# A channel gate between two LSTMs: statistics spread by TensorE, its 24 comparisons divided over VectorE, GpSimd and ScalarE

## The chip, the cores and the metric

The kernel runs on one core of a Trainium2 chip. The metric is the device time of one execution in microseconds (us). The five engines are named as in the profile: PE is TensorE (its weight loads are listed apart, as PEld), DVE is VectorE, ACT is ScalarE, POOL is GpSimd and SP is SyncE, which here only starts transfers.

## The reference

The input is a batch of 4 images with 256 channels of 64 x 64 pixels in float32. Two layers follow each other. The first adds a deformable 3 x 3 convolution of the normalized input and then an LSTM of width 256 over the pixels (`c_new = h * c + i * g`, three gates), which runs along the images' tokens. The second adds a gate over channels and again an LSTM. The change is about the gate of the second layer and the seams on both of its sides:

```python
def _L1_conv_ref(x, w, gamma, beta, running_mean, running_var):   # x: the normalized y, (b, c, h, w)
    b, c, h, wd = x.shape
    xf = x.reshape(b, c, h * wd)
    mean = xf.mean(-1)
    mx = xf.max(-1)
    std = jnp.std(xf, axis=-1, ddof=1)
    u = jnp.stack([mean, mx, std], axis=-1)
    med = jnp.median(u.reshape(b, -1), axis=-1)
    u = (u - med[:, None, None]) ** 3
    z = jnp.einsum('bck,ck->bc', u, w)
    z = (z - running_mean) * jax.lax.rsqrt(running_var + BN_EPS) * gamma + beta
    g = jax.nn.sigmoid(z)
    return x * g[:, :, None, None]

# --- layer 1 ---
x = x + _L1_conv_ref(_ln_c(x), ...)
t = _to_tokens(x)
t = t + _L1_ffn_ref(_ln_t(t), ...)
```

`_ln_c` normalizes each pixel over its 256 channels. For each image there are 256 x 3 = 768 statistics, and their median is needed before any gate can be computed. So the gate needs all of the first LSTM's output, and the second LSTM needs the gate.

## The kernel before

**Tiling.** The pixels of four images are cut into 128 tiles (`NTILE`), each of 128 lanes (32 for each image) by 256 channels. Each image's sequence of tokens is cut into 32 pieces that run side by side, one in each lane, so that one step of the LSTM handles one tile. A piece starts from a state that is guessed by some steps over the end of the piece before it; that the guess agrees with the state really reached is checked afterwards (`count_held`). `ORDER` (line 539) lists 144 steps: 16 that only warm the state up (`WARM`; of these the first 4, `FIRST`, are left out), and then the 128 tiles. Both the warm-up steps 4 to 15 and the last 12 steps (132 to 143) handle tiles 116 to 127.

**Order.** `Ordered` and `InOrder` (lines 391 to 430) tie each instruction to the one that the program issued before it on the same engine. The order in the code is therefore the order on every engine.

**First stage.** `sample_and_recur` (line 578) runs the sampling of the convolution, the first LSTM and the gate's statistics in numbered slots. The 576 (`PAIRS`) slots of sampling come first; the last steps of the LSTM go on for some 75 slots after that. In a slot each engine gets its fixed part (`core`), and then work from a list (`Spare`) that has become due and for which there is room. When two finished tiles of the LSTM have been normalized over channels (`styled`, line 857), ScalarE writes y and y squared into a buffer (`style`), VectorE adds both to sums over lanes (`lanes`) and takes the maximum (`highest`). Before slot 592 these buffers come from the pool "y", after it from `squares`: 40 tiles of 256 numbers that held the sampled rows, and that are used as 10 slots of four tiles. `free` lists the slots that can be had, and `highest` gives a slot back. The last pair, steps 142 and 143, goes through `ending` (line 902), in which TensorE adds up the sums over lanes into `pq`. `Gate.scaled` works out gamma divided by the square root of the running variance at slot 288.

**Gate.** `Gate.gates` (line 1429) follows the last step:

- It makes `u`, 128 lanes x 4 images x 6 numbers (two halves of the channels, three statistics). The lane is the channel.
- SyncE writes `u` to DRAM (`ud`) and reads each image's 768 numbers back to all 128 lanes (`ubs`, in the first 12 tiles of `squares`). Behind these five transfers in SyncE's queue stand loads for the second LSTM (`ring<-x2d`).
- Meanwhile ScalarE normalizes the 12 tiles 116 to 127 again, from `ring`, into `early` (line 1478), and VectorE runs `meanwhile()`: this is `count_held` (line 1097).
- Then, for each image and each of the 6 columns, the number of the 768 values that are not above the lane's own is counted. `OWN = 4` columns of each image are counted by VectorE, with one compare whose accumulator gives the count. For 2 columns ScalarE runs a sign and a square, each with an accumulator, and two small VectorE instructions turn these into the count (`net`, `both`, `le`).
- `idle` products with no use keep TensorE busy (`turn_over`): 4 of them from the next to last compare on, 10 behind the gate's last product.
- From the counts VectorE picks the candidates for the median, GpSimd takes the maximum over lanes (`partition_all_reduce`), and a few VectorE instructions lead to `z`. ScalarE takes the sigmoid, VectorE spreads it over each image's 32 lanes (`G2`), two products with the identity turn it over into PSUM (`pg`), and VectorE copies that to `gb`.

**Second stage.** `gated_lstm` (line 1115) is the second layer. `gated` (line 1147) multiplies the normalized tile by `gb`, adds it to the tile and takes statistics; for the first 12 tiles the normalized values are those in `early`. It begins with four tiles (line 1256 and after), their norm, and the first transposes (`xt`) on TensorE.

All of the waits above come from the tiles: the framework makes an instruction wait for the producers of what it reads and for the readers of what it overwrites.

Of the kernel before, what the change touches and what calls it, by code (L numbers as in the profile page):

```python
# [11 lines left out]
F32 = mybir.dt.float32  # L12
I32 = mybir.dt.int32
AF = mybir.ActivationFunctionType
ALU = mybir.AluOpType
# [4 lines left out]
P = 128  # L20
B, C, H, W = 4, 256, 64, 64
T = H * W
NC = C // P
# [63 lines left out]
def normalize(nc, out, x, rs, low, j, f=AF.Identity):  # L87
    nc.scalar.activation(out, x, f, scale=rs[:, j : j + 1], bias=low[:, j : j + 1])
# [489 lines left out]
def sample_and_recur(  # L578
# [241 lines left out]
        give("DVE", slot, 0.9 if n0 < LAST else 2.2, begin, urgent=n0 >= LAST, soon=lo < NB)  # L820


    now, free = {"slot": 0}, [*range(SQUARES)]
    taken = {"xn": 0, "y": 0, "ms": 0, "ys": 0, "cm": 0}

    def room(tag, n):
# [30 lines left out]
    def styled(b, p, slot):  # L857

        n = b * NB + 2 * p
        y, k = result(slot)  # L860
# [12 lines left out]

    def result(slot):

        if slot > PAIRS + 16:
            k = free.pop(0)
            return squares[:, 4 * k : 4 * k + 4].rearrange("p (q i) c -> p q i c", q=2), k
        taken["y"] += 1
        return yp.tile([P, 2, 2, C], F32, name="y", tag="y"), None  # L880

    def style(y, n, i):
        t = ORDER[n + i]
# [3 lines left out]
    def highest(y, k):  # L887
        nc.vector.tensor_max(gate.mx, gate.mx, y[:, 0])
        if k is None:
            taken["y"] -= 1  # L890
        else:
            free.append(k)

    def lanes(n, y, k, slot):
# [7 lines left out]
    def ending(slot):  # L902

        n = STEPS - 2
        (y, _), (both, _) = result(slot), result(slot)
# [8 lines left out]
        highest(y, 0)  # L914


    def step_slot(n):
# [137 lines left out]
    while s <= step_slot(STEPS) or not spare.empty():  # L1055
# [35 lines left out]
        if s + AHEAD < PAIRS:  # L1091
            gather(s + AHEAD)
        s += 1
    return lambda: count_held(nc, st, cnt, ((state["cell"], state["cguess"]), (state["h"], state["hguess"])))


def count_held(nc, st, cnt, pairs):

    for i, (end, guess) in enumerate(pairs):
        d = st.tile([P, NC, P], F32, name="dif", tag="hc")  # L1100
        nc.vector.tensor_sub(d, end, guess)
        nc.vector.tensor_mul(d, d, d)
# [12 lines left out]
def gated_lstm(tc, pools, const, weights, src, dst, cnt, gate):  # L1115
# [5 lines left out]
    nc = Ordered(tc.nc, pools["after"])  # L1121
    ident = const[0]
    Us, Vs, bs = weights
    rs_y, low_y, gb, early = gate
# [22 lines left out]
    def gated(b, j):  # L1147

        if b >= NBATCH:
            return  # L1150
        t, x = ORDER[b * NB] + j, ring[:, (b + 1) % 4, j]
        lo, hi = part(b, j)
        if j == lo:
            sts[b, lo] = sm.tile([P, 20, 6], F32, name="st", tag="sth")[:, : hi - lo]
        if b < 2:
            d = early[:, b * NB + j - FIRST]
        elif (b, j) in styles:
            d = styles.pop((b, j))
        else:
            d = yp.tile([P, C], F32, name="d", tag="y")  # L1160
            normalize(nc, d, x, rs_y, low_y, t)
        nc.vector.tensor_mul(d, d, gb)
        nc.vector.tensor_add(x, x, d)
        nc.vector.bn_stats(sts[b, lo][:, j - lo], x)

# [132 lines left out]
    def style(b, lo, n):  # L1298

        for j in range(lo, lo + n):  # L1300
            d = styles[b, j] = early[:, (b * NB + j - FIRST) % (2 * NB - FIRST)]
            normalize(nc, d, ring[:, (b + 1) % 4, j], rs_y, low_y, ORDER[b * NB] + j)

    def turned_over(b, p):
# [73 lines left out]
    put(*last)  # L1378
    assert not adds
    store(last[0], NB // 2, NB)  # L1380
    count_held(nc, st, cnt, ((cell, cguess), (h, hguess)))


class Gate:
# [15 lines left out]

    def scaled(self, nc, gamma, rvar):
        nc.vector.tensor_scalar(rvar, rvar, 1e-5, None, ALU.add)
        nc.vector.tensor_mul(self.params[1], gamma, inv_sqrt(nc, self.pools["small"], rvar, NC))

    def begin(self):
        nc = Ordered(self.tc.nc, self.pools["after"])
# [19 lines left out]
                        skip_group_check=True,  # L1426
                    )

    def gates(self, meanwhile):
# [8 lines left out]
        def each(v, n):  # L1438

            return v.unsqueeze(1).to_broadcast([P, B, n])  # L1440
# [22 lines left out]


        uf = u.rearrange("p i k s -> p i (k s)")
        ud = self.pools["dram"].tile([B, P * NU], F32, name="ud", tag="ud")
        nc.sync.dma_start(ud.rearrange("i (p s) -> p i s", s=NU), uf)
        ubs = []
        for i in range(B):
            ubs.append(space[:, i * P * NU : (i + 1) * P * NU])  # L1470
            nc.sync.dma_start(ubs[i], ud[i : i + 1].to_broadcast([P, P * NU]))


        OWN = 4
        minus = wk.tile([P, B, NU - OWN], F32, name="minus", tag="minus")
        nc.scalar.activation(minus, uf[:, :, OWN:], AF.Copy, scale=-1.0)

        early = self.pools["squares"][:, 3 * (B + 3) : 3 * (B + 3) + 2 * NB - FIRST]
        for n in range(FIRST, 2 * NB):
            normalize(nc, early[:, n - FIRST], self.pools["ring"][:, NB + n], self.rs, self.low, ORDER[n])  # L1480
        meanwhile()
        le = wk.tile([P, B, NU], F32, name="le", tag="le")
        net = wk.tile([P, B, NU - OWN], F32, name="net", tag="net")
        both = wk.tile([P, B, NU - OWN], F32, name="both", tag="both")
        cmp, *sgs = (space[:, i * P * NU : (i + 1) * P * NU] for i in range(B, B + 3))
        for i, ub in enumerate(ubs):
# [303 lines left out]
def metaformer_kernel(ctx: ExitStack, tc: tile.TileContext, a: dict, out: bass.AP):  # L1790
# [10 lines left out]
    with ExitStack() as main:  # L1801
# [53 lines left out]
        def gate_weights(queue):  # L1855
# [14 lines left out]
        held = sample_and_recur(  # L1870
            tc, pools, const, wconv, a["x"], table, plan, x1, x2, weights[0], cnt[:, 0], gt, *errands
        )
        gated_lstm(tc, pools, const, weights[1], x2, out, cnt[:, 1], gt.gates(held))


    held = fp.tile([P, 1], F32, name="held")
# [65 lines left out]
```

## Time and profile before

| | |
|---|---|
| median of 6 runs | 3088.23 us (3081.8 to 3092.93) |
| the profiled execution | 3090.72 us |
| its span in the profile | 3088.5 us |
| granted TensorE clock, mean | 0.987 of full speed |
| PE, PEld, DVE, ACT, POOL busy | 97%, 90%, 86%, 66%, 50% of the span |
| end of the sampling, by the last gather | 2153 us |
| last step of the first LSTM, its h | 2280.0 us |
| statistics `u` complete | 2291.66 us |
| first compare, last compare's end | 2299.01 us, 2315.88 us |
| first product with the gate | 2321.12 us |
| first transposes of the second LSTM | 2329.85 us |

Times inside the execution are counted from the start of the span. A line of the timeline gives the start, the length, the engine, the source line (420 for nearly all, since a helper issues them), the operation, the tile it writes and those it reads, the shapes, how many such instructions were merged, and in brackets how long the engine sat idle before it and what ended that. A group of instructions has its total, the mean of one in ns, and the idle time before them. The share of busy time over the whole span says little here: the gate is some 40 of 3088 us, and has limits of its own.

### The profile page before, as it was taken

The numbers are of one execution on the slowest core, as the hardware profiler recorded it, in microseconds if no ns is written. First come the engines' busy times: TensorE is split into PE (matmuls) and PEld (weight loads), VectorE is DVE, ScalarE is ACT, GpSimd is POOL, SyncE is SP. The second block draws the span as 40 slices with busy tenths as digits, with TensorE's granted clock in tenths as the row PEclk, the third lists the DMA queues.
The fourth block names the chain that finished last, engine by engine and source line by source line (L and its number), as shares of the span: only waits on it lengthen the run. The fifth ranks groups of instructions, "written<-read, shape, count | busy, mean of one in ns | idle before, by whom it ended". The sixth has DMA issues, their size and how long they took to land.

```text
span 3088.5 us, 61571 instructions
## 1 busy us (share of the span) xinstructions
PE 2992.6 (97%) x20252; PEld 2791.7 (90%) x20252; DVE 2669.2 (86%) x7864; ACT 2049.1 (66%) x5414; POOL 1552.0 (50%) x1577
## 2 busy tenths in 40 slices
PE   7978999999999999999999999999969999999998
PEld 6967999999999999999999999999968999999997
DVE  6768998989999999999999999999677777777774
ACT  6746566666777767767677777777775666666653
POOL 3357665555666666666666666666000123223221
PEclk9989999999999999999999999999979999999999
DMA  9999999999999999999999999998110245444442
GB/s 311 321 337 344 345 318 335 332 332 327 325 330 329 333 332 317 342 331 321 334 331 332 330 333 331 322 331 304 59 62 28 79 154 156 150 153 144 147 139 85
DMA packets 316024, 816.02 MB, mean 264 GB/s; under 512 B 100392, under 2 KB 104488, under 8 KB 313392
## 3 DMA queue, kind: packets, MB, share of 16 engines
q0 software_dynamic: 188288, 669.62, 62.1%
q1 hardware_dynamic: 124240, 139.95, 13.4%
q8 instruction: 163, 2.67, 0.3%
q10 hardware_dynamic: 3168, 2.43, 0.2%
q14 instruction: 165, 1.35, 0.1%
HBM read 694.91 MB, written 116.94 MB: 263 GB/s over the span
## 4 chain that ended last, share of the span: by engine, by line
PE 86%; issue 6%; DMA 3%; DVE 3%; ACT 1%; SPq 0%; POOL 0%; DVEq 0%; ACTq 0%; POOLq 0%
PE acc L420 30%; PE ga L420 14%; PE gacc L420 8%; PE gtr L420 8%; PE tr L420 8%; PE gb L420 7%; PE gga L420 4%; PE ggb L420 4%; DMA squares<-table,plan 2%; PE zacc L420 1%; DVE v L420 1%; PE xt L420 1%; PE ht L420 1%; DMA squares<-in_x_dram 1%; PE zga L420 1%
## 5 line engine op out<-in xcount | busy, mean ns | idle before, releaser
L420 POOL DMA_INDIRECT squares<-table,plan x1152 | 1308.7, 1136 | 671.2 <-DVE v L420 150.8
L420 DVE SCALAR_TENSOR_TENSOR v<-squares,plan,v 128x256 f32<-128x256 f32 x3456 | 1412.8, 476 | 24.9 <-ACT v L420 23.4
L420 PE MATMUL acc<-wconv,vt 128*128 128x256 f32 x4608 | 1094.7, 380 | 16.4 <-ACT vt L420 16.3
L420 PEld LDWEIGHTS acc<-wconv,vt 128*128 128x128 f32 x4608 | 832.2, 191 | 110.7 <-ACT vt L420 21.0
L420 ACT COPY vt<-tr 128x512 f32<-128x512 f32 x576 | 336.4, 584 | 524.5 <-PE tr L420 524.5
L420 ACT ACTIVATE v<-squares,plan 128x256 f32<-128x256 f32 x1152 | 531.0, 514 | 58.8 <-DMA squares<-table,plan 50.1
L420 PE MATMUL tr<-ident,v 128*128 128x128 f32 x2304 | 347.4, 273 | 12.2 <-DVE v L420 12.2
L420 PEld LDWEIGHTS tr<-ident,v 128*128 128x128 f32 x2304 | 274.2, 142 | 22.0 <-DVE v L420 9.9
L420 PEld LDWEIGHTS ga<-cm,Us 128*128 128x128 f32 x2240 | 270.9, 192 | 7.0 <-ACT ti L420 0.6
L420 PEld LDWEIGHTS ga<-h,Vs 128*128 128x128 f32 x2224 | 269.9, 192 | 6.3
L420 PE MATMUL ga<-cm,Us 128*128 128x128 f32 x2240 | 272.8, 275 | 0.4 <-ACT ti L420 0.4
L420 PE MATMUL ga<-h,Vs 128*128 128x128 f32 x2224 | 271.7, 275 | 0.0
L420 DVE TENSOR_TENSOR tg<-tg,ti 128x256 f32<-128x256 f32 x280 | 118.1, 422 | 155.7 <-ACT ti L420 154.3
L420 POOL DMA_DIRECT2D ring<-hd x240 | 144.4, 630 | 166.2 <-DMA hd<-sqh 158.2
L420 POOL DMA_DIRECT2D hd<-sqh x60 | 34.7, 578 | 383.5 <-DVE sqh L420 356.2
L420 ACT ACTIVATE tg<-gacc,bs 128x128 f32<-128x128 f32 x280 | 87.7, 364 | 174.6 <-PE gacc L420 174.6
L420 DVE TENSOR_TENSOR h<-to,th 128x256 f32<-128x256 f32 x278 | 117.0, 421 | 86.2 <-ACT th L420 86.2
L420 PEld LDWEIGHTS gacc<-h,plan 128*128 128x128 f32 x1112 | 143.9, 191 | 10.7 <-DVE h L420 3.9
L420 PEld LDWEIGHTS gb<-cm,Us 128*128 128x128 f32 x1120 | 145.8, 192 | 6.4
L420 PEld LDWEIGHTS gb<-h,Vs 128*128 128x128 f32 x1112 | 144.7, 192 | 6.3
L420 PE MATMUL gacc<-h,plan 128*128 128x128 f32 x1112 | 147.2, 275 | 2.0 <-DVE h L420 2.0
L420 ACT ACTIVATE th<-cell 128x256 f32<-128x256 f32 x256 | 108.4, 423 | 60.3 <-DVE cell L420 60.2
(221 smaller groups left out, 4638.2 us busy)
## 6 DMA issues: line engine op xcount, KB each, us to landing
squares<-table,plan POOLq DMA_INDIRECT x1152, 6.4
x1d<-ring SPq DMA_DIRECT2D x64, 256.0 KB
x2d<-ring SPq DMA_DIRECT2D x64, 256.0 KB
ring<-x2d SPq DMA_DIRECT2D x16, 1024.0 KB
out_dram<-ring SPq DMA_DIRECT2D x32, 512.0 KB
ring<-in_x_dram SPq DMA_DIRECT2D x62, 256.0 KB
hd<-sqh POOLq DMA_DIRECT2D x60, 256.0 KB, 2.7
ring<-hd POOLq DMA_DIRECT2D x240, 64.0 KB, 2.6
```

The lines of the kernel that those rows point to most:

```text
L420: ins = op(*args, **kw)
```

## The change

- **Spreading u.** The five transfers go. Each of the 24 columns of `u`, repeated over 128 columns, is transposed by TensorE, so that every lane gets the column's 128 numbers. Four of them fill a PSUM bank; the six banks are those of the LSTM ("acc", "acc", "tr", "tr", "ga", "gb"). ScalarE copies five of the banks to `squares`, VectorE the second.
- **Comparing.** `OWN` becomes 3: VectorE counts 3 columns of each image. For the other 3, GpSimd makes a tile of ones and zeros (in the pool "y", two buffers) and ScalarE sums it by a copy with an accumulator. The sign and square instructions and the two instructions that repaired their counts go.
- **Kept y.** The y of steps 132 to 143 goes to slots 4 to 9 of `squares`, which aren't given back; `early` refers to them. The list `free` has 4 slots instead of 10. The second set of 12 normalizations goes.
- **Differences.** The difference of the states and its square (four instructions) go from VectorE, where they stood behind `u`, to GpSimd, behind the last step. The two counts stay on VectorE, behind the bank's copy.
- **Constants.** `Gate.scaled` multiplies the weights and the running mean by the scale and subtracts the mean from beta (four more small instructions at slot 288); of the three instructions on `z` one is left.
- **From z to gb.** ScalarE takes the sigmoid straight into `G2`, spread over the lanes (two instructions; the two VectorE copies go). Two transposes take the place of the two products. ScalarE copies `pg` to `gb`, and the first tile is multiplied by `pg` in PSUM.

```diff
@@ sample_and_recur
-    now, free = {"slot": 0}, [*range(SQUARES)]
+    KEPT = WARM - FIRST
+    now, free = {"slot": 0}, [*range(SQUARES - KEPT // 2)]
...
+    early = {}
+    def result(n, slot):
         if slot > PAIRS + 16:
-            k = free.pop(0)
-            return squares[:, 4 * k : 4 * k + 4].rearrange("p (q i) c -> p q i c", q=2), k
+            if n >= STEPS - KEPT:
+                k = len(early) // 2 + SQUARES - KEPT // 2
+            else:
+                k = free.pop(0)
+            y = squares[:, 4 * k : 4 * k + 4].rearrange("p (q i) c -> p q i c", q=2)
+            if n >= STEPS - KEPT:
+                stay(n, y)
+                k = -1
+            return y, k
...
+    def stay(n, y):
+        for i in range(2):
+            early[ORDER[n + i]] = y[:, 0, i]
...
-        else:
+        elif k >= 0:
             free.append(k)
...
+    held = ((state["cell"], state["cguess"]), (state["h"], state["hguess"]))
+    apart = [differences(nc.gpsimd, st, i, pair) for i, pair in enumerate(held)]
+    return early, lambda: count_held(nc, st, cnt, apart)
+
+def differences(engine, st, i, pair):
+    d = st.tile([P, NC, P], F32, name="dif", tag=("hc", "tg")[i])
+    engine.tensor_sub(d, *pair)
+    engine.tensor_mul(d, d, d)
+    return d
@@ gated_lstm
-            d = early[:, b * NB + j - FIRST]
+            d = early[t]
...
-        nc.vector.tensor_mul(d, d, gb)
+        nc.vector.tensor_mul(d, d, pg if b == 0 and j == FIRST else gb)
@@ Gate.scaled
-        nc.vector.tensor_mul(self.params[1], gamma, inv_sqrt(nc, self.pools["small"], rvar, NC))
+        ws, scale, rmean, beta = self.params
+        nc.vector.tensor_mul(scale, gamma, inv_sqrt(nc, self.pools["small"], rvar, NC))
+        for k in range(NC):
+            nc.vector.tensor_scalar(ws[:, k], ws[:, k], scale[:, k : k + 1], None, ALU.mult)
+        nc.vector.tensor_mul(rmean, rmean, scale)
+        nc.vector.tensor_sub(beta, beta, rmean)
@@ Gate.gates
-        ud = self.pools["dram"].tile([B, P * NU], F32, name="ud", tag="ud")
-        nc.sync.dma_start(ud.rearrange("i (p s) -> p i s", s=NU), uf)
-        ubs = []
+        columns = u.rearrange("p i k s -> p (i k s)")
+        ub = space[:, 0 : B * P * NU].rearrange("p (g n) -> p g n", n=4 * P)
+        banks = [(at, self.pools[at]) for at in ("acc", "acc", "tr", "tr", "ga", "gb")]
+        for g, (tag, ps) in enumerate(banks):
+            bank = ps.tile([P, 4 * P], F32, name=f"u{tag}", tag=tag)
+            for n in range(4):
+                c = 4 * g + n
+                nc.tensor.transpose(
+                    bank[:, n * P : (n + 1) * P], columns[:, c : c + 1].to_broadcast([P, P]), ident
+                )
+            if g == 1:
+                nc.vector.tensor_copy(ub[:, g], bank)
+            else:
+                nc.scalar.copy(ub[:, g], bank)
+        meanwhile()
+        OWN = 3
+        le = wk.tile([P, B, NU], F32, name="le", tag="le")
+        cmp = space[:, B * P * NU : (B + 1) * P * NU]
         for i in range(B):
-            ubs.append(space[:, i * P * NU : (i + 1) * P * NU])
-            nc.sync.dma_start(ubs[i], ud[i : i + 1].to_broadcast([P, P * NU]))
-        OWN = 4
...
-        early = self.pools["squares"][:, 3 * (B + 3) : 3 * (B + 3) + 2 * NB - FIRST]
-        for n in range(FIRST, 2 * NB):
-            normalize(nc, early[:, n - FIRST], self.pools["ring"][:, NB + n], self.rs, self.low, ORDER[n])
-        meanwhile()
...
+            each_ub = space[:, i * P * NU : (i + 1) * P * NU]
             for j in range(OWN):
                 nc.vector.tensor_scalar(
-                    cmp, ub, uf[:, i, j : j + 1], None, ALU.is_le, ALU.add, accum_out=le[:, i, j : j + 1]
+                    cmp, each_ub, uf[:, i, j : j + 1], None, ALU.is_le, ALU.add, accum_out=le[:, i, j : j + 1]
                 )
-            for j in range(NU - OWN):
-                sg = sgs[j % 2]
-                c = slice(j, j + 1)
-                nc.scalar.activation(sg, ub, AF.Sign, bias=minus[:, i, c], accum_out=net[:, i, c])
-                nc.scalar.activation(sg, sg, AF.Square, accum_out=both[:, i, c])
+            for j in range(OWN, NU):
+                sg = self.pools["y"].tile([P, P * NU], F32, name="sg", tag="y")
+                nc.gpsimd.tensor_scalar(sg, each_ub, uf[:, i, j : j + 1], None, ALU.is_le)
+                nc.scalar.activation(sg, sg, AF.Copy, accum_out=le[:, i, j : j + 1])
...
-        nc.vector.tensor_add(net, net, both)
-        nc.vector.tensor_scalar(le[:, :, OWN:], net, -0.5, float(P * NU), ALU.mult, ALU.add)
...
-        nc.vector.tensor_sub(z, z, each(rmean, NC))
-        nc.vector.tensor_mul(z, z, each(scale, NC))
         nc.vector.tensor_add(z, z, each(beta, NC))
-        gt = wk.tile([P, B, NC], F32, name="gt", tag="gt")
-        nc.scalar.activation(gt, z, AF.Sigmoid)
         G2 = wk.tile([P, NC, P], F32, name="G2", tag="G2")
         pg = ps_ms.tile([P, C], F32, name="gp", tag="ms")
         for k in range(NC):
-            nc.vector.tensor_copy(
-                G2[:, k].rearrange("p (i r) -> p i r", i=B), gt[:, :, k : k + 1].to_broadcast([P, B, R])
+            nc.scalar.activation(
+                G2[:, k].rearrange("p (i r) -> p i r", i=B), z[:, :, k : k + 1].to_broadcast([P, B, R]), AF.Sigmoid
             )
-            nc.tensor.matmul(pg[:, k * P : (k + 1) * P], G2[:, k], ident, start=True, stop=True)
+            nc.tensor.transpose(pg[:, k * P : (k + 1) * P], G2[:, k], ident)
         turn_over(10)
         gb = self.pools["keep"].tile([P, C], F32, name="gb", tag="gb")
-        nc.vector.tensor_copy(gb, pg)
-        return self.rs, self.low, gb, early
+        nc.scalar.copy(gb, pg)
+        return self.rs, self.low, (pg, gb), early
```

More of the change, by code (lines that the diff above doesn't have):

```diff
@@ L859, in styled @@
         n = b * NB + 2 * p
-        y, k = result(slot)
+        y, k = result(n, slot)
         def other(slot):
@@ L872, in styled @@
         give("ACT", slot, 1.15, other, urgent=slot > PAIRS + 16)
-    def result(slot):
+    early = {}
+    def result(n, slot):
         if slot > PAIRS + 16:
-            k = free.pop(0)
-            return squares[:, 4 * k : 4 * k + 4].rearrange("p (q i) c -> p q i c", q=2), k
+            if n >= STEPS - KEPT:
[7 more added lines that the diff above has]
+            return y, k
         taken["y"] += 1
         return yp.tile([P, 2, 2, C], F32, name="y", tag="y"), None
+    def stay(n, y):
+        for i in range(2):
+            early[ORDER[n + i]] = y[:, 0, i]
     def style(y, n, i):
@@ L904, in ending @@
         n = STEPS - 2
-        (y, _), (both, _) = result(slot), result(slot)
+        (y, _), (both, _) = result(n, slot), result(0, slot)
         for i in range(2):
@@ L913, in ending @@
             gate.add(nc, both, (0,), (q,))
-        highest(y, 0)
+        highest(y, -1)
     def step_slot(n):
@@ L1093, in sample_and_recur, with count_held @@
         s += 1
[L1094 to L1102, printed above, removed]
+    held = ((state["cell"], state["cguess"]), (state["h"], state["hguess"]))
[6 more added lines that the diff above has]
+    return d
+def count_held(nc, st, cnt, apart):
+    for i, d in enumerate(apart):
         ok = st.tile([P, NC, P], F32, name="ok", tag="th")
@@ L1123, in gated_lstm @@
     Us, Vs, bs = weights
-    rs_y, low_y, gb, early = gate
+    rs_y, low_y, (pg, gb), early = gate
     st, cm_p, sm, ps_ms, yp, vp = (pools[n] for n in ("state", "cm", "small", "misc", "y", "v"))
@@ L1300, in style @@
         for j in range(lo, lo + n):
-            d = styles[b, j] = early[:, (b * NB + j - FIRST) % (2 * NB - FIRST)]
+            d = styles[b, j] = early[ORDER[FIRST + (b * NB + j - FIRST) % (2 * NB - FIRST)]]
             normalize(nc, d, ring[:, (b + 1) % 4, j], rs_y, low_y, ORDER[b * NB] + j)
@@ L1380, in gated_lstm @@
     store(last[0], NB // 2, NB)
-    count_held(nc, st, cnt, ((cell, cguess), (h, hguess)))
+    count_held(nc, st, cnt, [differences(nc.vector, st, i, x) for i, x in enumerate(((cell, cguess), (h, hguess)))])
 class Gate:
@@ L1427, in add, with gates @@
                     )
-    def gates(self, meanwhile):
+    def gates(self, early, meanwhile):
         nc = Ordered(self.tc.nc, self.pools["after"])
@@ L1465, in gates @@
         uf = u.rearrange("p i k s -> p i (k s)")
-        ud = self.pools["dram"].tile([B, P * NU], F32, name="ud", tag="ud")
-        nc.sync.dma_start(ud.rearrange("i (p s) -> p i s", s=NU), uf)
-        ubs = []
-        for i in range(B):
-            ubs.append(space[:, i * P * NU : (i + 1) * P * NU])
-            nc.sync.dma_start(ubs[i], ud[i : i + 1].to_broadcast([P, P * NU]))
-        OWN = 4
-        minus = wk.tile([P, B, NU - OWN], F32, name="minus", tag="minus")
-        nc.scalar.activation(minus, uf[:, :, OWN:], AF.Copy, scale=-1.0)
@@ L1478, in gates @@
-        early = self.pools["squares"][:, 3 * (B + 3) : 3 * (B + 3) + 2 * NB - FIRST]
-        for n in range(FIRST, 2 * NB):
-            normalize(nc, early[:, n - FIRST], self.pools["ring"][:, NB + n], self.rs, self.low, ORDER[n])
-        meanwhile()
[L1482 to L1485, printed above, removed]
@@ L1486, in gates @@
-        for i, ub in enumerate(ubs):
+        columns = u.rearrange("p i k s -> p (i k s)")
+        ub = space[:, 0 : B * P * NU].rearrange("p (g n) -> p g n", n=4 * P)
+        banks = [(at, self.pools[at]) for at in ("acc", "acc", "tr", "tr", "ga", "gb")]
+        own = []
+        for g, (tag, ps) in enumerate(banks):
[9 more added lines that the diff above has]
+                nc.scalar.copy(ub[:, g], bank)
@@ L1869, in metaformer_kernel @@
         )
-        held = sample_and_recur(
+        early, held = sample_and_recur(
             tc, pools, const, wconv, a["x"], table, plan, x1, x2, weights[0], cnt[:, 0], gt, *errands
         )
-        gated_lstm(tc, pools, const, weights[1], x2, out, cnt[:, 1], gt.gates(held))
+        gated_lstm(tc, pools, const, weights[1], x2, out, cnt[:, 1], gt.gates(early, held))
     held = fp.tile([P, 1], F32, name="held")
```

## The prediction

> **What bounds the kernel now.** I read the slices of the span first, then busy time by stretch around the hole in them, then the instructions in order of time inside it. In the slices TensorE is at nine tenths or more almost everywhere but in slice 30 (from about 2239 us, 77 us wide), where it falls to six tenths and its clock to seven:
>
> ```profile
> PE   7978999999999999999999999999969999999998
> PEclk9989999999999999999999999999979999999999
> ```
>
> That hole is the gate between the two LSTMs, all this change touches but for four tiny instructions. By stretch (start:end, length, then busy us and instructions of PE, PEld, DVE, ACT, POOL, then granted clock, DMA share, GB/s):
>
> ```profile
> 2277.50:2291.70 14.20, 8.92 (x46) 8.39 (x44) 10.36 (x44) 5.16 (x15) 0.00 (x0) 0.58 0.05 18
> 2291.70:2299.00 7.30, 0.00 (x0) 0.00 (x0) 2.41 (x8) 6.10 (x13) 0.00 (x0) 0.50 0.50 106
> 2299.00:2316.20 17.20, 2.38 (x5) 1.35 (x6) 16.58 (x34) 14.94 (x32) 0.00 (x0) 0.50 0.42 169
> 2316.20:2321.10 4.90, 4.41 (x13) 2.10 (x12) 3.03 (x16) 0.21 (x1) 0.88 (x3) 0.89 0.00 0
> ```
>
> Row two is a transfer (TensorE nothing, GpSimd nothing), row three is VectorE 16.6 of 17.2 us with ScalarE 14.9 beside it and GpSimd empty, row four a serial chain. The timeline (start, length, engine, instruction, idle before it) gives the corners:
>
> ```profile
> 2291.49 0.17 DVE L420 TENSOR_TENSOR u<-va,nwy 128x8 f32<-128x8 f32 x1
> ...
> 2291.69 0.37 SPq L420 DMA_DIRECT2D ud<-u  x1
> ...
> 2291.81 5.99 ACT L420 ACTIVATE squares<-ring,glow,grs 128x256 f32<-128x256 f32 x12
> ...
> 2299.01 1.01 DVE L420 TENSOR_SCALAR_CACHE_REDUCE squares<-squares,u 128x768 f32<-128x768 f32 x1 [4.73 <-DMA squares<-ud]
> ...
> 2316.20 0.26 DVE L420 TENSOR_SCALAR here<-le 128x24 f32<-128x24 f32 x2
> ...
> 2319.13 0.17 DVE L420 TENSOR_TENSOR z<-z,beta 128x8 f32<-128x8 f32 x1
> ...
> 2320.66 0.42 DVE L420 COPY gb<-gp 128x256 f32<-128x256 f32 x1 [0.73 <-PE gp L420]
> ```
>
> u is complete at 2291.66. Its way out to DRAM and back ends at 2299.01 (7.35 us). 16 compares of VectorE take until 2315.88, the two repairs of ScalarE's counts until 2316.20. From there to z's end are 3.10 us, from z to the first product with the gate (2321.12) another 1.82. Nothing of the second LSTM starts before that product, so each microsecond here is one of the end.
>
> **The change, part by part.**
>
> *Spreading u.* One transfer out and four back go; 24 transposes, five ScalarE copies and one VectorE copy come. At half clock eight such narrow products took 1.83 us of weight loads (pq, 2280.40), 0.23 each; the two pm transposes took 1.08 us from their operand's end to the next VectorE instruction, latency included. Columns 0 and 1 (mean, maximum) are ready earlier, so bank 1 is full after six more: 1.08 + 4 x 0.23 = 2.0, at 2293.7. VectorE copies it (0.69, the row gmx<- of 128x512), 2294.4, counts the held steps (two ok with their accumulator reads, 0.45 each, hidden under the transfer before and open now), and begins comparing at 2295.3, not 2299.0. Bank 5 is full after 22: 1.08 + 20 x 0.23 = 5.7, at 2297.35; ScalarE's copy (0.58, cm<-xt) ends at 2297.95. The lower bound is that the clock rises within these transposes: at 2313.82 it took 3.4 us of work until the 512-column products came at 0.43 instead of 0.86 us; that would save 0.7 us. The pq products ran 7 us at half clock without raising it, so I take none.
>
> *Twelve compares each.* VectorE keeps 12 of 1.057 us (1.012 and an accumulator read, start to start): 2295.3 + 12.7 = 2308.0. The other 12 go to GpSimd, each summed by a ScalarE copy. Two tiles rotate, and ScalarE has its bank copies ahead of the first sum, so GpSimd's third compare waits for that sum's end: 2298.0 + 0.85 = 2298.9 (128x768 activation 0.843). Ten more of p each and a last sum with its read, 0.95, give le at 2299.85 + 10p. No row shows a compare on GpSimd. The nearest rows are its copies:
>
> ```profile
> L420 POOL COPY early<-z 128x324 f32<-128x324 f32 x1 | 0.5, 457 | 0.9 <-ACT z L420 0.9
> L420 POOL COPY again<-squares 128x256 f32<-128x256 f32 x1 | 0.4, 397 | 0.1
> L420 POOL COPY squares<-again 128x256 f32<-128x256 f32 x1 | 0.5, 500 | 0.0
> L420 DVE TENSOR_SCALAR_CACHE_REDUCE squares<-squares,u 128x768 f32<-128x768 f32 x16 | 16.2, 1012 | 5.3 <-DMA squares<-ud 4.7
> ```
>
> From 397 ns at 256 to 457 at 324 elements is 0.88 ns an element, 0.85 us at 768; three times the slowest copy is 1.50. A compare with a per-lane operand is closest to the copy (one tensor in, one out), so near the lower end: p = 0.95, bounds 0.85 and 1.50. ScalarE's 0.85 a sum is just hidden under it. le is then at 2309.35 against 2316.20: **-6.85 us**; at 0.85, -7.85; at 1.50, -1.35.
>
> [...]
>
> *Kept y.* The 12 normalizations leave ScalarE (5.99 us). Alone that is worth nothing, they lay under the transfer; without that cover they would stand ahead of the bank copies and put 6 us on the path. In the tail, four pairs (steps 124 to 130) still rotate through the slots, now four; in the trace at most two are out at once (124's slot is freed at 2218, before 128's is taken at 2233), so nothing waits: 0.
>
> *Differences on GpSimd.* Four instructions of two 128x256 inputs, no such row; between one copy, 0.40, and twice the slowest, 1.0. They run in 2279.1 to about 2283. Behind them on GpSimd are only the compares, not due until 2294.4. What they may touch is VectorE's serial chain (h, the last maximum, the norm). Taking work away from VectorE gains nothing, since it lay under the transfer. I take +0.4 (one wait of a copy's length), bounds 0 and 1.0.
>
> [...]
>
> *Constants.* Two z instructions go (0.20 each, start to start): -0.4. Four small ones come at half of the sampling, 0.16 to 0.2 each on a VectorE that is nine tenths busy there: 0 to 0.8, I take +0.2.
>
> *From z to the first product.* Two sigmoids of 128x128 (tg's pair: 0.63, with waits 0.70), transposes instead of two-pass products (0.35 for the last against 0.70), product straight from PSUM: 1.1 instead of 1.82, **-0.72**. ScalarE's gb copy (0.5) lies under the first tile's product, addition and statistics (1.26).
>
> *Clock.* The first idle products start after VectorE's eleventh compare, 2306.9, reach full clock around 2310.3 and end around 2312.1; gp's transposes follow at 2312.9 and the next 20 products (8.75 us) end just as xt wants TensorE. If le comes over 2 us later, TensorE cools (it had dropped 2.2 us after its last wide product at 2277.7), four of these products take 0.86 instead of 0.43, and xt waits behind them: 0 as costed, +1.6 from p about 1.2 up.
>
> SP's queue loses five transfers, so the two loads of x2d behind them move up from 2296.28 to some 2285, into an idle DMA; their tiles are used tens of us later: 0. The reduction over lanes and the two clears on GpSimd stay behind the compares as they stood behind nothing; the clears are wanted around 2337.
>
> *Sum:* -6.85 - 0.40 - 0.72 + 0.40 + 0.20 = -7.4 us. The profiled execution took 3090.72 (span 3088.5, the rest around it), so 3083.3 in it; it lay 2.5 above the median of the runs, 3088.23, so the median becomes **3080.8**.
>
> **The rivals.**
> [...]
> - *Compares of the two engines exclude one another:* 12 x (1.057 + 0.95) = 24.1 from 2295.3, a last sum 0.95: le 2320.35, +4.15 - 0.52 = +3.6, **3091.8**. For: both read the same tile. Against: GpSimd's copies took 0.40 to 0.46 but for one.
> - *GpSimd walks its data twice, slower than before:* 2 x 3 x 0.403 = 2.42 a compare, le at 2324.05: +7.85 - 0.52 + 1.6 = +8.9, **3097**. It decides from p = 1.53 (no gain) and 2.15 (+6.2). For: the trace has no arithmetic at all on GpSimd. Against: the clears and copies, 0.33 to 0.50 for 256.
> - *The change doesn't do what it says:* the spread is replaced by a wait as long. It would need bank 1 at 2297.4, nearly three times the transposes' price; not given a chance of its own.
>
> **How the numbers follow.** Forecast 0.62, slower GpSimd without measurable change 0.12, exclusion 0.06, two walks 0.15, something unseen in the sampling's order 0.05 (0.02 faster, 0.03 slower). Telling apart from no change takes about 0.2%, 6.2 us. Faster 0.64, same 0.18, slower 0.18. Low end: p 0.85 with a rising clock lets VectorE's 2308.0 decide, -8.2 - 1.1 = -9.3, and 2 for the scatter of a median: 3077. High end: p 1.50 gives -1.35 - 0.52 + 1.6, about 3088, and up to 3092 it takes in the exclusion; the two walks stay out.
>
> **What would show it.** First VectorE compare 3.5 to 4 us after u; GpSimd compares start to start at 0.9 to 1.0 us; le decided by ScalarE's last sum some 1.5 us after VectorE's last compare; z to first product 1.1 us; 20 idle products at 0.43. A GpSimd compare over 1.1 us or VectorE compares over 1.06 make the forecast wrong.

## The result, and the profile after

The changed kernel took 3097.52 us in the median (3092.84 to 3101.4, 17 runs) against 3088.37 us before (37 runs): 9 us slower, ratio 1.0030 (95% interval 1.0024 to 1.0037). The profiled execution took 3093.52 us, its span is 3091.7 us. In it `u` was complete 6.7 us earlier than in the profile of before. That is scatter: e1 to e4 below, with the same code up to `u`, had it between 2286.86 and 2292.36 us. So the two are compared from the completion of `u` on, not from the start.

By stretch (busy us and instructions of PE, PEld, DVE, ACT, POOL, then granted clock, DMA share, GB/s, as before), from u's completion at 2284.93:

```profile
2284.90:2288.00 3.10, 3.02 (x14) 3.02 (x15) 1.34 (x5) 1.17 (x2) 0.56 (x1) 0.50 0.00 0
2288.00:2314.60 26.60, 7.58 (x20) 4.05 (x18) 12.28 (x26) 12.88 (x27) 25.62 (x12) 0.69 0.00 0
2314.60:2323.00 8.40, 1.08 (x3) 0.80 (x4) 1.91 (x11) 0.87 (x3) 0.91 (x3) 0.50 0.00 0
2323.00:2333.10 10.10, 10.10 (x20) 4.16 (x19) 9.23 (x34) 1.11 (x3) 0.00 (x0) 0.78 0.00 1
```

The first row, the spread of u, is as short as hoped. In the second GpSimd is busy 25.6 of 26.6 us, and VectorE, which bounded this stretch before, less than half. In the third, 8.4 us long, no engine is busy for even a quarter. The timeline shows the corners:

```profile
2284.76 0.17 DVE L420 TENSOR_TENSOR u<-va,nwy 128x8 f32<-128x8 f32 x1
...
2287.44 26.18 POOL L420 TENSOR_SCALAR sg<-squares,u 128x768 f32<-128x768 f32 x12 [11.79 <-issue]
...
2288.04 1.01 DVE L420 TENSOR_SCALAR_CACHE_REDUCE squares<-squares,u 128x768 f32<-128x768 f32 x1
...
2314.62 0.26 DVE L420 TENSOR_SCALAR here<-le 128x24 f32<-128x24 f32 x2 [13.68 <-ACT sg L420]
...
2315.16 0.20 DVE L420 TENSOR_REDUCE pick<-here 128x8 f32<-128x48 f32 x1
2319.65 0.39 POOL L420 PARTITION_ALL_REDUCE mid<-pick  x1 [6.03 <-issue]
...
2321.36 0.17 DVE L420 TENSOR_TENSOR z<-z,beta 128x8 f32<-128x8 f32 x1
...
2322.40 11.27 PE L420 MATMUL idle<-squares,ident 128*128 128x512 f32 x20
2322.64 0.37 ACT L420 COPY gb<-gp 128x256 f32<-128x256 f32 x1 [0.58 <-PE gp L420]
2323.05 0.42 DVE L420 TENSOR_TENSOR squares<-squares,gp 128x256 f32<-128x256 f32 x1 [1.52 <-ACT gb L420]
...
2334.78 1.99 PE L420 MATMUL gacc<-cm,plan 128*128 128x256 f32 x8 [0.67 <-ACT cm L420]
```

Twelve compares of GpSimd take 26.18 us; VectorE waits 13.68 us for the last sum. The picks are ready at 2315.36, yet the reduction over lanes starts 4.3 us later; GpSimd had been idle for 6.03 us, waiting for nothing that the profile shows. The same step began 0.1 us after the picks before the change, and the 20 idle passes behind the gate (`idle`) took 8.75 us there, not 11.27:

```profile
2316.74 0.20 DVE L420 TENSOR_REDUCE pick<-here 128x8 f32<-128x48 f32 x1
...
2317.04 0.37 POOL L420 PARTITION_ALL_REDUCE mid<-pick  x1 [163.12 <-DVE pick L420]
...
2320.46 8.75 PE L420 MATMUL idle<-squares,ident 128*128 128x512 f32 x20
...
2331.46 1.99 PE L420 MATMUL gacc<-cm,plan 128*128 128x256 f32 x8 [0.68 <-ACT cm L420]
```

The starts and ends of these lines, and of the first projection of the second LSTM (`gacc`), cut the gate into five stages; "the picks" are taken from their first instruction (`here<-le`), which waits for the last count. All are in us and come from one profiled execution each; the runs that follow are listed with them:

| | u to first compare | to the picks | to z | to first product | to projection | u to projection |
|---|---|---|---|---|---|---|
| before | 7.35 | 17.19 | 3.10 | 1.82 | 10.34 | 39.80 |
| changed | 3.11 | 26.58 | 6.91 | 1.52 | 11.73 | 49.85 |
| e1 all on VectorE | 3.11 | 25.62 | 2.76 | 1.36 | 10.35 | 43.20 |
| e2 signs | 3.11 | 18.30 | 2.76 | 1.36 | 10.35 | 35.88 |
| e3 no reduction on GpSimd | 3.11 | 26.58 | 3.50 | 1.53 | 11.75 | 46.47 |
| e5 three ways | 2.45 | 16.55 | 2.76 | 2.81 | 10.34 | 34.91 |
| e6 and early products | 1.78 | 16.45 | 2.76 | 3.65 | 10.35 | 34.99 |
| e7 idle products later | 3.11 | 26.58 | 6.78 | 1.36 | 10.33 | 48.16 |
| e8 normalized again | 3.12 | 24.22 | 2.76 | 1.53 | 11.55 | 43.18 |
| e9 best | 2.61 | 16.44 | 2.75 | 1.78 | 10.32 | 33.90 |
| e10 copy behind product | 3.11 | 18.31 | 2.76 | 0.96 | 10.34 | 35.48 |
| e11 differences on VectorE | 4.61 | 17.45 | 2.69 | 1.51 | 10.33 | 36.59 |

The gate itself lost 10.05 us: -4.24 spread, +9.39 compares, +3.81 picks to z, -0.30 z to product, +1.39 product to projection. That is the 9 us of the medians within their scatter.

e7, e8, e10 and e11 ran once each and are read by these stages alone, and e4, which also ran once, by GpSimd's rows; e5 to e8, e10 and e11 ran on chips on which the kernel before took 3172 to 3210 us, so no total of theirs is compared with those of the other runs. One of e9's 11 executions took 4015.96 us at a granted clock of 0.73 and one of e6's 12 took 3201.99 us; the ratios leave these two out.

### The profile page after: what moved, and what is told of

Its sections match the earlier page's. It is cut to its first block, busy times and chain, and to the rows that moved or that the text cites. A ratio compares the mean times of both kernels' runs of the same rounds, so it can differ in the third digit from the quotient of the medians.

```text
span 3091.7 us, 61601 instructions
## 1 busy us (share of the span) xinstructions
PE 2996.1 (97%) x20274; PEld 2794.3 (90%) x20274; DVE 2663.4 (86%) x7850; ACT 2040.5 (66%) x5400; POOL 1572.9 (51%) x1593
## 4 chain that ended last, share of the span: by engine, by line
PE 92%; DVE 3%; DMA 2%; ACT 1%; POOL 1%; issue 1%; DVEq 0%; ACTq 0%; POOLq 0%
PE acc L420 31%; PE ga L420 16%; PE tr L420 8%; PE gacc L420 8%; PE gtr L420 8%; PE gb L420 8%; PE gga L420 4%; PE ggb L420 4%; DMA squares<-table,plan 2%; PE zacc L420 1%; PE xt L420 1%; PE ht L420 1%; POOL sg L420 1%; PE zga L420 1%; PE zgb L420 1%
## 5 line engine op out<-in xcount | busy, mean ns | idle before, releaser
L420 PEld LDWEIGHTS acc<-wconv,vt 128*128 128x128 f32 x4608 | 831.6, 190 | 108.7 <-ACT vt L420 19.2
```

The costliest lines, as they stand in the source:

```text
L420: ins = op(*args, **kw)
```

## The experiments

**Which engine compares (e1, e2).** e1 sets `OWN = 6`. e2 gives the two columns back to ScalarE:

```diff
-        OWN = 3
+        OWN = 4
...
+        nc.scalar.activation(minus, uf[:, :, OWN:], AF.Copy, scale=-1.0)
...
-                nc.gpsimd.tensor_scalar(sg, each_ub, uf[:, i, j : j + 1], None, ALU.is_le)
-                nc.scalar.activation(sg, sg, AF.Copy, accum_out=le[:, i, j : j + 1])
...
+                nc.scalar.activation(sg, each_ub, AF.Sign, bias=minus[:, i, c], accum_out=net[:, i, c])
+                nc.scalar.activation(sg, sg, AF.Square, accum_out=both[:, i, c])
...
+        nc.vector.tensor_add(net, net, both)
+        nc.vector.tensor_scalar(le[:, :, OWN:], net, -0.5, float(P * NU), ALU.mult, ALU.add)
```

> All 24 compares on VectorE (OWN = 6), the rest as changed. [...] Then VectorE's 24 x 1.057 = 25.4 us follow the first compare at 3.1 us after u, the reduction starts at once (from the picks' first instruction to z 2.7 us), z to the first product 1.5, product to the first projection 10.3: 43.0 us from u to the projection against 49.85 changed and 39.80 before, so about 3091 us. Rival: the reduction's wait doesn't come from the compares on GpSimd; then from the picks to z stay 6.9 us, and the time is about 3095 us.

> Comparisons divided as before the change (4 columns of an image on VectorE, 2 as sign and square on ScalarE), everything else as changed. Theory 1 (all of the loss is GpSimd's compares and what follows from them): VectorE ends 3.1 + 16.9 = 20.0 us after u, ScalarE 5.6 + 8 x 1.9 = 20.9, repaired counts at 21.3, then 2.7 + 1.5 + 10.3: 35.8 us from u to the first projection, 4.0 less than before, about 3084 us. Rival: the other parts (kept y, differences on GpSimd, two readers of PSUM) cost something that the gate's stages don't show; then not below 3088 us although the interval is 35.8.

e1 took 3090.07 us against 3087.29 before on its chip, ratio 1.0011 (1.0001 to 1.0022), with 43.20 us for the gate where 43.0 were expected. The reduction followed its picks at once:

```profile
2315.59 0.26 DVE L420 TENSOR_SCALAR here<-le 128x24 f32<-128x24 f32 x2
...
2316.47 0.40 POOL L420 PARTITION_ALL_REDUCE mid<-pick  x1 [38.85 <-DVE pick L420]
```

GpSimd had stood idle for 38.85 us, and the reduction was released by the picks, not by "issue". e2 took 3081.66 us, ratio 0.9985 (0.9976 to 0.9994): 35.88 us where 35.8 were expected. So the change without GpSimd's share of the compares, taken as a whole, makes the kernel faster, and that share cost 14.0 us of the gate (49.85 less 35.88) against signs on ScalarE: 8.3 in the compares, 4.2 from the picks to z, 1.5 behind that. VectorE alone is slower than before, but faster than with GpSimd's help.

**What the reduction waited for (e3).** The reading to be tested was that the 6.03 us come with the reduction on GpSimd when it stands close behind other work there. Before the change it stood behind 163.12 us of idle time and began 0.1 us after its picks; now it stands behind the twelve compares. No row shows what fills the 6.03 us. e3 takes the reduction from GpSimd:

```diff
-        nc.gpsimd.partition_all_reduce(
-            mid.rearrange("p n i -> p (n i)"), pick.rearrange("p n i -> p (n i)"), P, bass_isa.ReduceOp.max
...
+        nc.tensor.transpose(ends[0 : 2 * B, 0], pick.rearrange("p n i -> p (n i)"), ident)
...
+        nc.vector.tensor_reduce(most[0 : 2 * B], ends[0 : 2 * B, 0], AX.X, ALU.max)
+        nc.tensor.transpose(
+            ends[:, 1, 0 : 2 * B], most[0 : 2 * B].to_broadcast([2 * B, P]), ident[0 : 2 * B, 0 : 2 * B]
         )
+        nc.vector.tensor_copy(mid.rearrange("p n i -> p (n i)"), ends[:, 1, 0 : 2 * B])
```

> As changed, but the maximum over lanes is taken by two transposes of TensorE, a VectorE reduction and a copy, without GpSimd. Theory 1: from the picks to z 6.9 falls to about 3.3 us (four short instructions at some 1.2 us for 0.5), the compares stay at 26.6; about 3094 us. [...]

Picks to z took 3.50 us instead of 6.91, with the compares unchanged at 26.58; 3095.16 us, ratio 1.0027 (1.0015 to 1.0039). TensorE's 20 idle passes behind the gate were as slow as in the changed kernel (11.29 us; product to projection 11.75), so the clock wasn't the cause. The wait belongs to the reduction on GpSimd: in e3 the next instruction there, a clear (`cguess`), began at 2319.58, as the last compare ended. e5, below, is the other half: with compares on GpSimd that end early, the wait is gone. The runs thus show some 6 us between GpSimd's work and a reduction behind it (6.03 here, 5.76 in e4). What fills them no run shows.

**The price of a GpSimd instruction (e4).** Its twelve instructions were changed by image; the counts of those columns then are not the reference's.

```diff
-                nc.gpsimd.tensor_scalar(sg, each_ub, uf[:, i, j : j + 1], None, ALU.is_le)
-                nc.scalar.activation(sg, sg, AF.Copy, accum_out=le[:, i, j : j + 1])
+                n = P * NU // (2 if j == OWN + 1 else 1)
+                if i == 0:
+                    nc.gpsimd.tensor_scalar(sg[:, 0:n], each_ub[:, 0:n], uf[:, i, j : j + 1], None, ALU.is_le)
+                elif i == 1:
+                    nc.gpsimd.tensor_scalar(sg[:, 0:n], each_ub[:, 0:n], uf[:, i, j : j + 1], None, ALU.subtract)
+                elif i == 2:
+                    nc.gpsimd.tensor_scalar(sg[:, 0:n], each_ub[:, 0:n], 1.0, None, ALU.is_le)
+                else:
+                    nc.gpsimd.tensor_copy(sg[:, 0:n], each_ub[:, 0:n])
+                nc.scalar.activation(sg[:, 0:n], sg[:, 0:n], AF.Copy, accum_out=le[:, i, j : j + 1])
```

> GpSimd's twelve instructions changed, three to an image, of 768, 384 and 768 elements: image 0 is_le with a per-lane operand, image 1 a subtraction with a per-lane operand, image 2 is_le with a constant, image 3 a plain copy; the counts of these columns are then not those of the reference. Theory A (the price is that of any scalar operation on GpSimd): 2.18, 1.2, 2.18 us in images 0 to 2, copy 0.85 and 0.5. Theory B (the compare alone is slow): subtraction near the copy, 0.9 to 1.2. Rival (VectorE excludes GpSimd): the prices fall when VectorE's compares are over, some 13 us after its first.

GpSimd's groups by form (busy us, mean ns; the first holds both is_le and subtraction):

```profile
L420 POOL TENSOR_SCALAR sg<-squares,u 128x768 f32<-128x768 f32 x4 | 8.8, 2209 | 12.3 <-issue 11.8 <-ACT sg L420 0.6
L420 POOL TENSOR_SCALAR sg<-squares 128x768 f32<-128x768 f32 x2 | 4.3, 2129 | 0.0
L420 POOL TENSOR_SCALAR sg<-squares,u 128x384 f32<-128x384 f32 x2 | 2.5, 1242 | 0.0
L420 POOL COPY sg<-squares 128x768 f32<-128x768 f32 x2 | 1.6, 825 | 0.3 <-ACT sg L420 0.3
L420 POOL COPY sg<-squares 128x384 f32<-128x384 f32 x1 | 0.5, 502 | 0.3 <-ACT sg L420 0.3
```

Theory A holds. A subtraction costs what a compare costs, a constant operand 4% less. An element is (2209 - 1242) / 384 = 2.5 ns for arithmetic and (825 - 502) / 384 = 0.84 ns for a copy. Why arithmetic goes at a third of the speed of a copy no run shows. The copies followed the compares without a gap here; the reduction came 5.76 us after the last copy. The exclusion of VectorE and GpSimd falls with the changed kernel's own rows, in which GpSimd's price is the same beside VectorE's compares, to 2301, and alone after them (minimum, median and maximum in ns):

```profile
L420 POOL TENSOR_SCALAR sg<-squares,u x12: 2200/2201/2219, 2287.4 to 2311.4; 128x768 f32<-128x768 f32 x12
```

**Three engines by their prices (e5, e6, e9).** e5 gives each image's last column to GpSimd, five to ScalarE's signs and 15 to VectorE, moves the counts of held steps ahead of the bank's copy, and copies gb behind the first product. e6 adds two products without use while u is completed; e9 starts the idle products two compares earlier.

```diff
+        SIGNED = [(i, 0) for i in range(B)] + [(0, 1)]
...
+        meanwhile()
...
+            own = [j for j in range(NU - 1) if (i, j) not in SIGNED]
+            for j in own:
...
+            j = NU - 1
...
+            nc.gpsimd.tensor_scalar(sg, each_ub, uf[:, i, j : j + 1], None, ALU.is_le)
...
+            nc.vector.tensor_mul(d, d, pg)
+            nc.scalar.copy(gb, pg)
@@ e6, ahead of u's mean
+        for _ in range(2):
+            nc.tensor.matmul(early_idle, ident, self.pools["squares"][:, RING - 2 :], start=True, stop=True)
@@ e5 and e6, ahead of the idle products
+        nc.tensor.matmul(idle[:, 0, 0:2], ident, le[:, B - 1, NU - 3 : NU - 1], start=True, stop=True)
@@ e9, in its place
+        nc.tensor.matmul(idle[:, 0, 0:2], ident, le[:, B - 1, 1:3], start=True, stop=True)
```

> 15 compares on VectorE, 5 columns as sign and square on ScalarE, 4 compares on GpSimd with ScalarE's sums; the counts of the held steps stand ahead of the bank's copy; gb is copied behind the first product with PSUM. [...]

> As the division three ways, and two products without use on TensorE while VectorE completes u. Theory (TensorE's clock is what fills the banks slowly): four passes of 0.86 us end as u does, the clock is then full, bank 5 is copied at about 3.6 us after u instead of 5.6, bank 1 at 1.9; ScalarE ends at 16.9, VectorE at 1.9 + 15.9 = 17.8, counts at 18.3: 32.4 us from u to the projection, 0.9 less than without. Rival: the products come late or don't raise the clock: no gain, or up to 1 us lost.

> The division three ways with the two early products, and the idle products behind the gate's compares start two VectorE compares earlier, so that gp's transposes find TensorE free. Theory: z to the first product falls from 3.65 to 0.95 us (the transposes stood behind eight idle passes), the rest as in the run before: 32.3 us from u to the projection against 39.8 before the change, 7.5 us less, ratio 0.9976. Rival: the first product waits for both readers of the bank whatever their order; then 1.4 us and 32.8.

For e5 33.3 us were expected from u to the projection, added up from measured times: 2.3 to the first compare, the counts ready at 19.2, then 2.8 to z, 0.95 to the first product and 10.35 to the projection, with GpSimd's compares done at 11.2, early enough for the reduction to follow its picks at once; 37.3 if it waited 4 us again.

e5 and e6 ran on a chip on which the kernel before took 3187.14 us and scattered widely; ratios 0.9978 (0.9953 to 1.0002, so not settled) and 0.9954 (0.9925 to 0.9983). The counts came 0.2 and 0.1 us earlier than expected, 19.0 and 18.2 us after u, but the gate missed its 33.3 and 32.4 us. In e5 GpSimd's fourth compare ended 6.38 us ahead of the reduction, and the picks released it at once:

```profile
2395.80 2.20 POOL L420 TENSOR_SCALAR sg<-squares,u 128x768 f32<-128x768 f32 x1 [2.19 <-ACT sg L420]
2404.39 0.40 POOL L420 PARTITION_ALL_REDUCE mid<-pick  x1 [6.38 <-DVE pick L420]
```

The loss lies behind z. From there to the first product it took 2.81 and 3.65 us, since gp's transposes stood behind idle products that had been started by the last compares, and which now ran when the gate wanted TensorE (`gp`). e9 took 3081.09 us, ratio 0.9982 (0.9973 to 0.9992), and 33.90 us. It missed its 32.3: the idle passes still ended 0.8 us late, most of them at half clock (a granted 0.59 from 2306.0 to 2312.4), and the clock, which the early products (`warm`) were to raise, rose only 1.7 us after u (2289.06), so the banks filled later than in e6:

```profile
2285.49 3.62 PE L420 MATMUL warm<-squares,ident 128*128 128x512 f32 x4
2288.90 1.91 PE L420 MATMUL uacc<-ident,u 128*128 128x128 f32 x8
2290.61 1.12 PE L420 MATMUL utr<-ident,u 128*128 128x128 f32 x8
...
2306.19 6.18 PE L420 MATMUL idle<-squares,ident 128*128 128x512 f32 x8
2312.22 0.38 PE L420 MATMUL gp<-ident,G 128*128 128x128 f32 x2
```

The first eight transposes took 1.91 us, the next eight 1.12. In e6, with the same early products, the granted clock was full 0.9 us ahead of u (the weight loads of the six transposes that followed u took 0.63 us, against 1.14 in e5), and the first compare came 1.78 us after u instead of 2.61. e9 and e2 both took less time than both kernels; their difference in time is within the intervals.

**The clock (e7).**

```diff
-        nc.tensor.matmul(idle[:, 0, 0:2], ident, le[:, B - 1, 0:2], start=True, stop=True)
+        nc.tensor.matmul(idle[:, 0, 0:2], ident, le[:, B - 1, NU - 2 :], start=True, stop=True)
```

> As changed, but the idle products wait for the last columns' sums instead of VectorE's last compares. Theory (TensorE cools during 16 us without work, and the 20 idle products behind the gate then take 11.3 us): product to projection falls from 11.73 to about 10.35 us, the rest as changed, 48.5 us from u to the projection. Rival: the projection waits for something else; 11.7 us stay.

Product to projection fell to 10.33 us; the 20 passes behind the gate took 8.75 instead of 11.27 us:

```profile
2427.65 8.75 PE L420 MATMUL idle<-squares,ident 128*128 128x512 f32 x20
```

**Kept y (e8).** To e2's kernel, `normalize` of the 12 tiles into `early` was added behind the bank copies.

> The division by signs (4 columns on VectorE, 2 on ScalarE), and the 12 normalizations done a second time behind the banks' copies. Theory (the transfer that covered them is gone): ScalarE starts its signs 6.0 us later, counts at 24.4 instead of 18.3 + 3.1 = 21.4 less what VectorE leads, so 5.5 to 6 us more from u to the projection, 41.5 to 42 us. Rival: VectorE decides and covers them: under 2 us more.

43.18 us, above the 42 expected and 7.3 more than e2: 5.9 in the compares, as costed, and most of the rest because TensorE's clock was low again (product to projection 11.55, the 20 idle passes 11.09, with a granted clock of 0.52 from 2423.0 to 2428.5). With the transfer gone and e2's division, keeping y is worth this.

**Two readers of PSUM (e10).** To e2's kernel, with ScalarE's copy issued behind the first product:

```diff
+            nc.vector.tensor_mul(d, d, pg)
+            nc.scalar.copy(gb, pg)
...
-        nc.scalar.copy(gb, pg)
```

> The division by signs, and ScalarE's copy of gb issued behind the first product instead of ahead of it. Theory (the product waits for ScalarE's copy of the same PSUM tile because that copy was issued first): z to the first product falls from 1.36 to 0.95 us, the copy then starts as the product ends, 35.5 us from u to the projection. Rival: the product waits for TensorE's transposes alone; 1.36 us stay.

0.96 us, as expected, with ScalarE's copy now behind the product:

```profile
2413.52 0.42 DVE L420 TENSOR_TENSOR squares<-squares,gp 128x256 f32<-128x256 f32 x1 [0.96 <-PE gp L420]
2413.98 0.37 ACT L420 COPY gb<-gp 128x256 f32<-128x256 f32 x1 [0.88 <-DVE squares L420]
```

Whichever is issued first of these two readers, the other waits for it: the profile names ScalarE's copy as what released the product in the changed kernel, and the product as what released the copy here.

**Differences (e11).** To e2's kernel, with `differences(nc.vector, ...)` called inside `meanwhile()`.

> The division by signs, and the two differences and squares of the held states back on VectorE behind u. Theory of the prediction (GpSimd's differences hold up VectorE's chain by 0.4 us): from the last cell to u 12.2 to 12.3 us instead of 12.6 to 12.7, h 0.42 us long instead of 0.62; the four instructions, 1.8 us, fit into VectorE's wait of 1.6 us for the first banks, so the first compare comes at most 0.3 us later. [...]

This expectation had two misses. The way to u: the last `cell` to u took 12.56 us, 0.13 less than e2's 12.69, not 0.4. GpSimd's first difference and h do overlap in e2, and h takes 0.62 instead of 0.43 us:

```profile
2279.76 0.73 POOL L420 TENSOR_TENSOR dif<-cell,cguess 128x256 f32<-128x256 f32 x1 [125.68 <-DVE cell L420]
2280.15 0.62 DVE L420 TENSOR_TENSOR h<-to,th 128x256 f32<-128x256 f32 x1 [0.48 <-ACT th L420]
```

Nor is the 0.13 us the price of the differences in the changed kernel. There they ran on GpSimd too, h took 0.62 us too, and the way from the last `cell` to u was 12.56 us, as it was before the change without them. In these two and in e11 the norm's first instruction (`nm`) followed ScalarE's earlier work without a gap, 2.75 us after the cell's start, so the longer h was covered. Only where h's transposes (`ht`) were longer as well, 0.66 instead of 0.41 us in e2 (0.66 also before the change, at a granted clock of 0.50), did `nm` slip, to 2.83. In the changed kernel other waits cover the longer h.

The place: `meanwhile()` stands behind the bank's copy, not in the wait ahead of it, so the first compare came 1.5 us later, not 0.3. ScalarE's share covered half of that; the gate was 0.7 us longer.

## Why the prediction was wrong

Forecast were 3080.8 us, 7.4 less than before, with a range of 3077 to 3092; measured were 3097.52, 9 more than before, with a gate 10.05 us longer.

- **The failed step: "near the lower end: p = 0.95, bounds 0.85 and 1.50".** The compare cost 2.18 us start to start, which over ten of them is 12.3 us. The extrapolation of the copies was right (0.85 foreseen for 768 elements, 0.825 in e4). Wrong was the step from a copy to arithmetic: it goes at 2.5 ns an element instead of 0.84. The upper bound was also taken from copies, so the range couldn't hold it. The trace of before had no arithmetic on GpSimd, as the text itself noted for its slow rival, and the term was taken from the nearest rows all the same. With it the part that was to gain 6.85 us lost 5.15: the counts came 29.69 us after `u` instead of 24.54.
- **A wait put at nothing: "The reduction over lanes and the two clears on GpSimd stay behind the compares as they stood behind nothing".** The reduction began 6.03 us after the last compare, and 4.3 us of that were on the path. That the wait belongs to a reduction close behind other work on GpSimd is shown by e1, e3 and e5. The text went by rows, and no row of the profile shows what fills this time.
- **From z to the first product, 1.1 us:** 1.52. The transposes were as costed; the product waited 0.4 us for ScalarE's copy (e10), which the text had put under the first tile's work.
- **The clock:** the bound "+1.6 from p about 1.2 up" came in at +1.39 (e7).
- **The spread:** 3.11 us to the first compare where 3.64 were worked out; VectorE began to copy bank 1 at 1.63 us after `u`, not 2.0. Gain 4.24.
- **Two z instructions** -0.4: e1 and e2 have 2.76 from picks to z against 3.10. **Differences** +0.4: nothing in the changed kernel, 0.13 in e2 (e11). **Constants** +0.2: no run tried them by themselves. **Kept y**, worth nothing under the transfer: not tried by itself; once the transfer is gone, 7.3 us (e8).

With p = 2.18 in place of 0.95, the wait ahead of the reduction, the wait for ScalarE's copy and the clock, the working of the prediction gives -7.4 + 12.3 + 4.2 + 0.4 + 1.4 = +10.9, less the 0.4 and 0.2 for differences and constants, which are not in the gate, and 0.3 at the start of the compares: +10.0, as measured for the gate (10.05).

The rival with two walks over the data gave 3097 us, which is the time measured, but only in part by its own mechanism: its 2.42 us a compare put 7.85 us on the counts, the real 2.18 put 5.15, and the wait ahead of the reduction, which it didn't know, made up the rest. Its number was luck; whether GpSimd walks its data twice no run shows.

## What to carry to other kernels

An engine that stood idle has no prices in the profile: its own copies and clears did not bound its arithmetic here (0.825 against 2.20 us), so give it a share only after one run that measures the price. Count the waits that a moved instruction pulls along and that no row shows, such as the 6 us ahead of the reduction here: with GpSimd idle for 38.85 us (e1) none of them was on the path, behind its compares 4.3 us were. When a stage is balanced over engines, its idle products, copies and loads must be timed anew, since each was placed for the old end.

## What the runs showed of the hardware

- GpSimd took 0.825 us to copy 128x768 numbers and 2.20 us for a compare or subtraction of them; VectorE's compare with a count took 1.01 us.
- The reduction over lanes began 5.8 to 6.0 us after other work on GpSimd that ended shortly before it (6.03 in the changed kernel, 5.76 in e4, 5.90 in e7), and as soon as its operand was there after 6.38 us or more of idle time (e5, e1, e2). A change from compares to copies (e4) or to a clear (e3) left no such gap.
- Beside GpSimd's difference of two tiles VectorE's h took 0.62 us instead of 0.43 (e2, e11); VectorE's compare with a count stayed at 1.01 us beside GpSimd's compares.
- TensorE at half clock (a granted 0.50 from 2284.9 to 2288.0 in the changed kernel) filled a bank with four transposes in 0.86 us. The granted clock became full 4.9 us after the first of the 22 transposes that followed `u` in the changed kernel, when they were all but done, and 3.1 in e11, where the last but one bank took 0.49 us. With wide passes ahead of the transposes it became full 2.7 us after the first of these in e6 and 5.3 in e9. So the wide passes alone did not fix when it rose. Products of four columns (`pq`) kept TensorE busy for 7.4 of 7.7 us before the change (from 2280.1) without raising it from half.
